# Output weights asked for earlier in the opening, and by another queue in the second half

## The chip, the cores and the metric

The kernel runs on one core of a Trainium2 chip, in one launch. A core has TensorE (PE: matrix products; its weight loads are PEld), VectorE (DVE), ScalarE (ACT), GpSimd (POOL) and SyncE (SP). SP, ACT and POOL also issue DMAs, each on a queue of its own; the transfers of all three run on the same 16 DMA engines. The metric is the device time in microseconds (us), of which lower is better.

## The reference, cut to what matters

The input x has 64 batches of 32 tokens of 512 values. Two layers follow one another, each added to its input:

```python
W = weights[condition]                       # one 32 x 32 matrix per batch
x = x + einsum('bct,bcd->bdt', x, W)         # mixes the 32 tokens of a batch

q = rope(rmsnorm(x @ Wq.T))                  # 32 heads of 128
k = rope(rmsnorm(x @ Wk.T))                  # 8 heads of 128, each for 4 heads of q
v = x @ Wv.T
k_all = concat(k_cache[block_table], k)      # 16 pages of 32 cached keys, and the 32 new ones
v_all = concat(v_cache[block_table], v)
probs = softmax(where(valid, q @ k_all.T / sqrt(128), -1e30))
x = x + (probs @ v_all) @ Wo.T               # Wo: 512 x 4096
```

All of it is in float32. The tables of pages and the lengths are inputs of the run.

## The kernel before, in words

**Tiling.** The heads are cut into two halves (16 heads of q, 4 of k and v in each). The tokens are cut into 16 tiles of 128, which is four batches each. A *step* is one tile in one half: steps 0 to 15 are the first half, 16 to 31 the second (`NT` is 16). The four batches of a step and the four heads of k make 16 *slots*, numbered 0 to 15; in each slot TensorE computes the scores of one batch and head against the 512 cached keys (`ps`, L570), ScalarE takes the exponential (`pr`), and one slot later TensorE multiplies with the values (`po`, L628). Around this, each step prepares the next one: in slots 3 to 7 TensorE projects k and q of the next step (`pp_k`, `pp_q`, L401), and VectorE normalizes and rotates them (a chain of some eight instructions for each q) and writes them to `rows`. In slots 9 and 11 SP *spreads* them by DMA from `rows` to `q_cols` (batches 0 to 2 of the step) and `q_last` (batch 3), four DMAs per batch, L465. In slots 8 and 9 TensorE does the output projection of the step before (`pout`, L516), with the output weights `wo`. In slots 14 and 15 it mixes and turns the x of the step after the next (`pmix`, `px1t`); ScalarE copies the result to `x1t` and stores it to memory for the second half (`x1t_d`, L368, issued by ACT). At the start of a step come the scores and values against the new keys (`psn`, L588, and `pnv`, L612): `psn` reads the queries and keys of all four batches of its step, so it needs the whole spread.

**The opening.** Step 0 has no step before it. All that it needs is written out in a fixed order of its own: projections, two batches of scores and the first fills, up to slot 4 of step 0, where the loop takes over.

**Keys and values.** The keys of a batch come as 16 pages, one DMA of 64 KB for each page, issued by SP (`k_t`, L291), into two buffers; `Batch(...)` issues them, two batches ahead. VectorE copies them head by head to `kh` (L563), which frees the buffer. The values come in four chunks of 256 KB for a batch, each gathered by an indirect DMA of POOL (`raw`, L315) into three buffers; ScalarE masks a chunk into `v` (L328), which frees its buffer for the next gather.

**Output weights.** `wo` of one half is four tiles of 1 MB. `load_parts` asks for half a tile, in two DMAs of 256 KB, each of which fills 32 partitions (L249). There is one set of tiles for both halves: the second half's weights may come only when the last projection of the first half has read the tile.

**Fallback.** The exponentials are taken without subtracting a maximum; at the end a count of the denominators decides whether a second, exact pass runs. It doesn't in the runs shown.

**Order.** SP and TensorE do their work in the order in which the program writes it. ACT, VectorE and POOL are ordered by a scheduler, after the opening. Each engine issues and waits in its order: what stands behind a waiting instruction waits too. The table that places the loads of `wo` by step and slot is:

```python
        output_weights = {
            (0, 4): (0, 1),
            (0, 5): (2, 3),
            (0, 6): (4, 5),
            (1, 4): (6,),
            (1, 5): (7,),
            (NT, 10): (0,),
            (NT + 1, 2): (1,),
            (NT + 1, 4): (2,),
            (NT + 1, 5): (3, 4),
            (NT + 1, 6): (5, 6),
            (NT + 1, 7): (7,),
        }
```

Of the kernel before, what the change touches and what calls it, by code (L numbers as in the profile page):

```python
# [20 lines left out]
B, S, HID = 64, 32, 512  # L21
# [7 lines left out]
NT = B // BT  # L29
NHH = 2  # L30
GH = HK // NHH
# [24 lines left out]
def cond_resid_paged_attention_kernel(  # L56
# [23 lines left out]
    nc = tc.nc  # L80
# [101 lines left out]
    def run(exact):  # L182

        with ExitStack() as pools:
            steps_of(exact, pools)

    def steps_of(exact, pools):
# [46 lines left out]
        def load_w(kind, hh, g=0, part=slice(0, 4), eng=nc.sync):  # L234
            if kind == "q":
                src = wq[:, (hh * QH + g * REP) * D : (hh * QH + (g + 1) * REP) * D]
            elif kind == "o":
                src = wo[(hh * QH + g * REP) * D : (hh * QH + (g + 1) * REP) * D, :]
            else:
                src = (wk if kind == "k" else wv)[:, hh * GH * D : (hh + 1) * GH * D]  # L240
            if part.start == 0:
                wt[kind, hh, g] = wpool.tile(
                    [P, 4, 512], F32, tag=f"w{kind}{g}", name=f"w{kind}{g}_{hh}_{uid}"
                )
            t = wt[kind, hh, g]
            if kind == "o" and not exact:
                src = src.rearrange("(h j p) e -> h p j e", h=REP, p=S)
                for h in range(part.start, part.stop):
                    nc.sync.dma_start(t[h * S : (h + 1) * S, :, :], src[h])  # L249
                return  # L250
            eng.dma_start(t[:, part, :], src.rearrange("(c p) e -> p c e", p=P)[:, part, :])

        def load_parts(which, hh, at):

            if 0 <= at < 2 * len(which):
                load_w(which[at // 2][0], hh, which[at // 2][1], slice(at % 2 * 2, at % 2 * 2 + 2))

        def load_cond_weights(t, eng=nc.sync, kind=mybir.EngineType.SP):
            _, number = nc.values_load_multi_w_load_instructions(
# [234 lines left out]
        def k_b(st):  # L494
            to_columns(st, GH)
# [58 lines left out]
        def queries(ba, g):  # L554
            return columns(ba.st, ba.bt)[:, g, :]

        def head_keys(ba, g, eng=None):

            k = work.tile([P, NPP, PSIZE], F32, tag="kh", name=f"kh_{ba.name}_{g}", bufs=4)
            if eng is nc.scalar:  # L560
                nc.scalar.copy(k, ba.k_raw[:, :, g, :])
            else:
                last["dve"] = nc.vector.tensor_copy(k, ba.k_raw[:, :, g, :]).ins  # L563
            ba.k[g] = k.rearrange("p j r -> p (j r)")

        def scores(ba, g):

            ps = ps_s.tile([P, VC, P], F32, tag="ps", name=f"ps_{ba.name}_{g}")
            for c in range(VC):
                nc.tensor.matmul(  # L570
                    ps[:, c, :],
                    ba.k[g][:, c * P : (c + 1) * P],
                    queries(ba, g),
                    start=True,
                    stop=True,
                )
            pr = work.tile([P, VC, P], F32, tag="pr", name=f"pr_{ba.name}_{g}", bufs=3)
            last["act"] = nc.scalar.activation(pr, ps, AF.Exp, scale=SCALE).ins  # L578
            ba.pr[g] = pr
# [241 lines left out]
        head_keys(batch, 2, nc.scalar)  # L821
        head_keys(batch, 3, nc.scalar)
        scores(batch, 0)
        after = Batch(first, 2)
        k_b(first)
        for c in (0, 1):
# [34 lines left out]
        def pieces(st):  # L861
            do = {
                2: (rot_tables,),
                3: (k_a,),
                4: ((q_a, 0),),
                5: ((q_a, 1),),
                6: ((q_a, 2),),
                7: ((q_a, 3),),
                9: ((spread, (0, 1, 3)),),
                11: ((spread, (2,)),),  # L870
                13: (v_a,),
            }
            if st is second:
                do[2] = do[3] = do[13] = ()
            return do
# [14 lines left out]
        def next_values():  # L890
# [7 lines left out]

        x1_a(steps[2])
        load_cond_weights(2)  # L900
        output_weights = {
            (0, 4): (0, 1),
            (0, 5): (2, 3),
            (0, 6): (4, 5),
            (1, 4): (6,),
            (1, 5): (7,),
            (NT, 10): (0,),
            (NT + 1, 2): (1,),
            (NT + 1, 4): (2,),
            (NT + 1, 5): (3, 4),  # L910
            (NT + 1, 6): (5, 6),
            (NT + 1, 7): (7,),
        }
        for st in steps:
            ahead = steps[st.n + 1] if st.n + 1 < len(steps) else None
            beyond = steps[st.n + 2] if st.n + 2 < len(steps) else None
            fill = pieces(ahead) if ahead else {}
            for bt in range(0 if st.n else 1, BT):
                this, after = batch, None
                n = st.n * BT + bt + 2  # L920
                if n < NHH * NT * BT:
                    after = Batch(steps[n // BT], n % BT)
                    unfilled += [(after, c) for c in range(VC)]
                for g in range(GH):
                    slot = bt * GH + g
                    if st.n or slot > GH:
                        scores(this, g)
                    if slot == 0:
                        new_scores(st)
                    if slot in (1, 3):  # L930
                        new_values(st, slot - 1)
                    if slot < GH and valued is not None:
                        values(*valued)
                    for piece in fill.get(slot, ()):
                        if isinstance(piece, tuple):
                            piece[0](ahead, piece[1])
                        else:
                            piece(ahead)
                    if slot in (8, 9) and st.n:
                        out_proj(steps[st.n - 1], slice((slot - 8) * QH // 2, (slot - 7) * QH // 2))  # L940
                    if slot == 9:
                        if st.n:
                            new_ot(st)
                        for ba in turned:
                            turn(ba)
                        turned = []
                        if 0 < st.n < NT // TRIG - 1:
                            tmp = work.tile(
                                [P, 3, TRIG * HD], F32, tag="w1", name=f"trig_{st.n}", bufs=1
                            )  # L950
                            with tc.issue_after(last["dve"]), tc.issue_after(last["act"]):
                                angles((st.n + 1) * TRIG, tmp)
                    if slot == 10 and st.n:
                        store(steps[st.n - 1])
                    if st.n and beyond:
                        if slot == 6 and not beyond.hh:
                            load_cond_weights(beyond.t)
                        if slot == 11:
                            x1_a(beyond)
                    if slot == 13 and beyond:  # L960
                        x1_t(beyond)
                    if slot == 14 and beyond:
                        x1_c(beyond)
                    if slot == 15 and beyond:
                        x1_b(beyond)
                    if slot == 1 and st.n == NT:
                        count(0)
                    for at in output_weights.get((st.n, slot), ()):
                        load_parts([("o", i) for i in range(GH)], st.hh, at)
                    if st.n in (NT - 2, NT - 1):  # L970
                        load_parts(
                            [("k", 0), ("q", 0), ("q", 1), ("q", 2), ("q", 3), ("v", 0)],
                            1,
                            slot - 5 + (st.n - NT + 2) * BT * GH,
                        )
                    for _ in range({1: 0, GH: 2}.get(slot, 1)):
                        if unfilled and (g or unfilled[0][0] is this):
                            next_values()
                    if slot >= GH and valued is not None:
                        values(*valued)  # L980
                    valued = this, g
                    if g == 1 and bt != 1:
                        for ba in turned:
                            turn(ba)
                        turned = []
                    if later is not None:
                        head_keys(later, g)
                turned.append(this)
                batch, later = later, after
# [75 lines left out]
```

## Time and profile before

| what | value |
|---|---|
| time, median of 3 runs | 2191.49 us (2189.07 to 2192.82) |
| the profiled execution: its time | 2190.95 us |
| the profiled execution: its span, first to last instruction | 2189.2 us |
| PE busy | 2151.3 us, 98% |
| VectorE, ScalarE, POOL busy | 55%, 40%, 37% |
| DMA: mean rate over the span | 164 GB/s |
| granted TensorE clock, mean | 0.992 |
| SP's issues of k_t, q_cols and q_last, wo | 2048, 372 and 124, 32 |
| POOL's gathers raw | 512 |

A line of a timeline gives the start and the length in us, the engine, the line of the kernel, the operation, what it writes and reads, how many instructions are merged, and in brackets the idle time before it and what ended that. A line of the waits gives the engine and line that waited, who released it, the sum in us, the number of waits and the longest. SPq, ACTq and POOLq are the issuing sides of these engines. The names end in `_x` where buffers have numbers.

### The profile page before, as it was taken

Reading aid. Unit: us, or ns where it says so; the run is one execution under the profiler, and the core shown is the slowest. Engines: PE = TensorE matmul, PEld = TensorE weight load, DVE = VectorE, ACT = ScalarE, POOL = GpSimd, SP = SyncE. Lnnn points to the kernel's source line nnn. Section 1 sums busy time; section 2 is a strip of 40 time slices with the busy share of each in tenths; the row PEclk is TensorE's granted clock in tenths of the full one; section 3 lists DMA queues with packets and bytes.
Section 4 is the critical chain, followed back from the end, with each engine's and each line's share of the span. In section 5 each row is a group of like instructions: output and inputs, shape, how many; then the busy total and the mean of one; then the engine's idle time right before and its main releaser. Section 6 shows DMA issues by size and latency. Waiting matters only on the chain.

```text
span 2189.2 us, 41546 instructions
## 1 busy us (share of the span) xinstructions
PE 2151.3 (98%) x12970; PEld 1500.0 (69%) x12970; DVE 1199.7 (55%) x2881; ACT 867.3 (40%) x1574; POOL 806.1 (37%) x1008
## 2 busy tenths in 40 slices
PE   8879999999999999999999999999999999999998
PEld 5657766677766777667777667777667776667775
DVE  5555566655565545556545656445556445656442
ACT  3434444444333443334443334443334443334441
POOL 4433333433343333334333434333334334334330
PEclk9989999999999999999999999999999999999999
DMA  7656555555555555556856865555555655555652
GB/s 227 175 157 176 150 154 145 167 163 159 161 144 158 161 169 154 153 151 189 252 166 173 206 169 160 169 162 163 147 162 160 173 162 155 151 162 161 175 153 62
DMA packets 387863, 358.77 MB, mean 164 GB/s; under 512 B 54737, under 2 KB 316897, under 8 KB 387633
## 3 DMA queue, kind: packets, MB, share of 16 engines
q1 hardware_dynamic: 342912, 215.10, 35.0%
q0 software_dynamic: 41712, 136.66, 21.8%
q10 hardware_dynamic: 3008, 4.25, 0.5%
q8 instruction: 106, 1.74, 0.3%
q14 instruction: 125, 1.02, 0.2%
HBM read 302.59 MB, written 12.58 MB: 144 GB/s over the span
## 4 chain that ended last, share of the span: by engine, by line
PE 97%; DMA 1%; SPq 1%; issue 0%; ACT 0%; DVE 0%; ACTq 0%; DVEq 0%
PE po_x L628 22%; PE ps_x L570 21%; PE pout_x L516 20%; PE pp_q_x L401 20%; PE pp_v_x L401 5%; PE pp_k_x L401 5%; PE pnv_x L612 2%; PE psn_x L588 2%; PE pmix_x L357 1%; SPq L465 0%; DMA wq_x<-in_wq_dram 0%; SPq L291 0%; PE px1t_x L365 0%; DMA x1t_d<-x1t_x 0%; DMA w_sel<-in_w_cond_dram,cond 0%
## 5 line engine op out<-in xcount | busy, mean ns | idle before, releaser
L315 POOL DMA_INDIRECT raw_x<-in_vc_dram,v_row x512 | 539.8, 1054 | 840.3 <-ACT v_x L328 772.5
L578 ACT ACTIVATE pr_x<-ps_x 128x512 f32<-128x512 f32 x512 | 305.8, 597 | 833.8 <-PE ps_x L570 774.1
L628 PEld LDWEIGHTS po_x<-v_x,pr_x 128*128 128x128 f32 x4096 | 517.0, 192 | 125.6 <-issue 115.2
L628 PE MATMUL po_x<-v_x,pr_x 128*128 128x129 f32 x4096 | 552.3, 278 | 1.1 <-issue 1.1
L401 PE MATMUL pp_q_x<-wq_x,x1t_x 128*128 128x512 f32 x1024 | 463.4, 595 | 4.3 <-DMA wq_x<-in_wq_dram 4.3
L516 PE MATMUL pout_x<-wo_x,ot_x 128*128 128x512 f32 x1024 | 450.2, 592 | 0.0
L570 PE MATMUL ps_x<-q_cols_x,kh_x 128*128 128x128 f32 x3072 | 406.9, 275 | 13.1 <-DMA q_cols_x<-rows_x 12.6
L570 PEld LDWEIGHTS ps_x<-q_cols_x,kh_x 128*128 128x128 f32 x3072 | 377.4, 192 | 29.8 <-issue 28.3
L328 ACT ACTIVATE v_x<-raw_x,valid 128x512 f32<-128x512 f32 x512 | 363.0, 716 | 9.5 <-DMA raw_x<-in_vc_dram,v_row 9.5
L516 PEld LDWEIGHTS pout_x<-wo_x,ot_x 128*128 128x128 f32 x1024 | 189.7, 190 | 214.3 <-issue 214.0
L401 PEld LDWEIGHTS pp_q_x<-wq_x,x1t_x 128*128 128x128 f32 x1024 | 186.0, 192 | 190.2 <-issue 185.7
L563 DVE COPY kh_x<-k_t_x 128x512 f32<-128x512 f32 x506 | 206.2, 417 | 195.7 <-PE ps_x L570 159.1
L646 DVE TENSOR_TENSOR nv_x<-po_x,nv_x 128x258 f32<-128x258 f32 x256 | 108.4, 423 | 322.8 <-PE po_x L628 311.0
L418 POOL TENSOR_TENSOR rs_q_x<-ms_q_x,minus_half 128x4 f32<-128x4 f32 x128 | 140.7, 1099 | 176.2 <-DVE ms_q_x L416 176.2
L411 ACT ACTIVATE sq_q_x<-pp_q_x 128x512 f32<-128x512 f32 x128 | 76.6, 598 | 272.9 <-PE pp_q_x L401 171.2
L570 PE MATMUL ps_x<-q_last_x,kh_x 128*128 128x128 f32 x1024 | 135.1, 275 | 0.0
L524 DVE TENSOR_TENSOR acc_x<-pout_x,acc_x 128x512 f32<-128x512 f32 x32 | 22.1, 692 | 199.5 <-PE pout_x L516 199.5
L570 PEld LDWEIGHTS ps_x<-q_last_x,kh_x 128*128 128x128 f32 x1024 | 124.6, 192 | 0.0
L401 PE MATMUL pp_k_x<-wk_x,x1t_x 128*128 128x512 f32 x256 | 116.1, 596 | 0.0
L401 PE MATMUL pp_v_x<-wv_x,x1t_x 128*128 128x512 f32 x256 | 115.2, 592 | 0.0
L415 DVE TENSOR_REDUCE ms_q_x<-sq_q_x 128x4 f32<-128x512 f32 x128 | 86.6, 676 | 49.9 <-ACT sq_q_x L411 48.0
L649 DVE TENSOR_TENSOR o_x<-nv_x,rden 128x256 f32<-128x256 f32 x256 | 108.5, 424 | 6.5
(105 smaller groups left out, 1464.5 us busy)
## 6 DMA issues: line engine op xcount, KB each, us to landing
k_t_x<-in_kt_dram SPq DMA_DIRECT2D x2048, 64.0 KB
q_cols_x<-rows_x SPq DMA_DIRECT2D x372, 80.0 KB
q_last_x<-rows_x SPq DMA_DIRECT2D x124, 80.0 KB
raw_x<-in_vc_dram,v_row POOLq DMA_INDIRECT x512
wo_x<-in_wo_dram SPq DMA_DIRECT2D x32, 256.0 KB
acc_x<-in_x_dram SPq DMA_DIRECT2D x16, 256.0 KB
x1t_d<-x1t_x ACTq DMA_DIRECT2D x16, 256.0 KB
acc_d<-acc_x SPq DMA_DIRECT2D x16, 256.0 KB
```

What stands on the lines that cost most here:

```text
L315: nc.gpsimd.indirect_dma_start(out=raw.rearrange("p g d -> p (g d)"), out_offset=None, in_=vc, in_offset=bass.IndirectOffsetOnAxis(ap=v_ro ...
L328: nc.scalar.activation(v_bufs[b % 2][:, c, :, 0:D], raw, AF.Copy, scale=ok)
L401: nc.tensor.matmul(pp, st.x1t[:, c, :], w[:, c, :], start=(c == 0), stop=(c == KC - 1))
L415: nc.vector.tensor_reduce(ms, sq, AX.X, ALU.add)
L418: nc.gpsimd.tensor_tensor(rs, ms, minus_half, ALU.pow)
L516: nc.tensor.matmul(st.po, st.ot[:, i, :], wt["o", st.hh, i // 4][:, i % 4, :], start=(i == 0), stop=(i == QH - 1),)
L563: last["dve"] = nc.vector.tensor_copy(k, ba.k_raw[:, :, g, :]).ins
L570: nc.tensor.matmul(ps[:, c, :], ba.k[g][:, c * P : (c + 1) * P], queries(ba, g), start=True, stop=True,)
L578: last["act"] = nc.scalar.activation(pr, ps, AF.Exp, scale=SCALE).ins
L628: nc.tensor.matmul(ba.po[:, g % 2, :], ba.pr[g][:, c, :], ba.v_t[:, c, g, :], start=(c == 0), stop=(c == VC - 1),)
L646: nc.vector.tensor_tensor(t, ba.po, t, ALU.add)
L649: nc.vector.tensor_tensor(ba.o[:, both, :], t[:, :, 0:D], rd.unsqueeze(2).to_broadcast([P, 2, D]), ALU.mult,)
```

## The change

The loads of the output weights are placed anew. In the first half SP still issues them: parts 0 to 2 directly after the opening's first score (that is between the pages of batches 1 and 2), parts 3 to 5 ahead of the loop (between the pages of batches 2 and 3), and parts 6 and 7 in slots 4 and 5 of step 1, as before. In the second half POOL issues them instead of SP, one part at a time: in slots 10, 13 and 15 of step 16 and in slots 1, 3, 4, 5 and 6 of step 17. `load_parts` and `load_w` take the issuing engine as an argument.

```diff
-                    nc.sync.dma_start(t[h * S : (h + 1) * S, :, :], src[h])
+                    eng.dma_start(t[h * S : (h + 1) * S, :, :], src[h])
...
-        def load_parts(which, hh, at):
+        def load_parts(which, hh, at, eng=nc.sync):
 
             if 0 <= at < 2 * len(which):
-                load_w(which[at // 2][0], hh, which[at // 2][1], slice(at % 2 * 2, at % 2 * 2 + 2))
+                kind, g = which[at // 2]
+                load_w(kind, hh, g, slice(at % 2 * 2, at % 2 * 2 + 2), eng)
+
+        outputs = [("o", g) for g in range(GH)]
...
         scores(batch, 0)
+        for at in (0, 1, 2):
+            load_parts(outputs, 0, at)
         after = Batch(first, 2)
...
         load_cond_weights(2)
-        output_weights = {
...
-        }
+        for at in (3, 4, 5):
+            load_parts(outputs, 0, at)
+        second_outputs = [(0, 10), (0, 13), (0, 15), (1, 1), (1, 3), (1, 4), (1, 5), (1, 6)]
...
-                    for at in output_weights.get((st.n, slot), ()):
-                        load_parts([("o", i) for i in range(GH)], st.hh, at)
+                    if st.n == 1 and slot in (4, 5):
+                        load_parts(outputs, 0, slot + 2)
+                    if (st.n - NT, slot) in second_outputs:
+                        at = second_outputs.index((st.n - NT, slot))
+                        load_parts(outputs, 1, at, nc.gpsimd)
```

More of the change, by code (lines that the diff above doesn't have):

```diff
@@ L900, in steps_of @@
         load_cond_weights(2)
-        output_weights = {
[L902 to L912, printed above, removed]
-        }
+        for at in (3, 4, 5):
+            load_parts(outputs, 0, at)
+        second_outputs = [(0, 10), (0, 13), (0, 15), (1, 1), (1, 3), (1, 4), (1, 5), (1, 6)]
         for st in steps:
```

## The prediction

> **What bounds the kernel now.** I read the page's busy line first, then the waits of TensorE, then the timelines of TensorE and of SP's queue around the longest wait.
>
> ```profile
> PE 2151.3 (98%) x12970; PEld 1500.0 (69%) x12970; DVE 1199.7 (55%) x2881; ACT 867.3 (40%) x1574; POOL 806.1 (37%) x1008
> ```
>
> TensorE is busy for 98% of the span, so only its idle time, some 38 us, can be won. Its waits say where the large pieces lie:
>
> ```profile
> PE ps_x L570 <- DMA q_cols_x<-rows_x: 12.6, 1, 12.6
> PE psn_x L588 <- DMA q_cols_x<-rows_x: 5.3, 1, 5.3
> PE pp_q_x L401 <- DMA wq_x<-in_wq_dram: 4.3, 1, 4.3
> PE pmix_x L357 <- DVE bd L799: 2.4, 1, 2.4
> ```
>
> The first two belong to one place, the border of steps 0 and 1. No wait of TensorE is later than 125.25 us, and step borders repeat every 67.1 us in the first half and 65.9 us in the second: the second half has nothing to give. In TensorE's timeline the place is:
>
> ```profile
> 103.17 1.06 PE L628 MATMUL po_x<-v_x,pr_x 128*128 128x129 f32 x8
> 116.85 2.05 PE L570 MATMUL ps_x<-q_cols_x,kh_x 128*128 128x128 f32 x8 [12.62 <-DMA q_cols_x<-rows_x]
> 118.83 1.10 PE L588 MATMUL psn_x<-q_cols_x 128*32 128x128 f32 x4
> 125.25 0.61 PE L588 MATMUL psn_x<-q_cols_x 128*32 128x128 f32 x2 [5.33 <-DMA q_cols_x<-rows_x]
> ```
>
> From step 0's pmix (100.09) to the next pp_k (136.44) takes 36.35 us; the same pieces a step later (189.54 to 203.57) take 14.03. The place costs 22.3 us: 17.95 of waiting, the rest mostly the clock (window 120 to 125.2: granted 0.50). Both waits are for the spread of queries that SP issues, and SP's queue shows why it is late:
>
> ```profile
> 73.54 11.02 SPq L249 DMA_DIRECT2D wo_x<-in_wo_dram  x12
> ...
> 89.02 2.63 SPq L291 DMA_DIRECT2D k_t_x<-in_kt_dram  x3
> ...
> 106.51 1.36 SPq L291 DMA_DIRECT2D k_t_x<-in_kt_dram  x3
> ...
> 112.69 5.06 SPq L465 DMA_DIRECT2D q_cols_x<-rows_x  x8
> 117.80 2.49 SPq L465 DMA_DIRECT2D q_last_x<-rows_x  x4
> 120.38 2.43 SPq L465 DMA_DIRECT2D q_cols_x<-rows_x  x4
> ```
>
> SP's own waits between 60 and 140 us, and the issue on ACT that they name:
>
> ```profile
> SPq L291 <- DMA x1t_d<-x1t_x: 14.7, 1, 14.7
> ```
>
> ```profile
> 104.10 0.36 ACTq L368 DMA_DIRECT2D x1t_d<-x1t_x  x1
> ```
>
> Pages of batch 4 stop after four issues (86.98, then three from 89.02) and go on at 106.51. The built program's list of waits explains it: DMAs of SP and ACT take eight completion semaphores in turn, and each waits until the last DMA on its semaphore has landed. The fifth page drew the one that x1t_d of step 2 uses. That store leaves ACT at 104.10, after TensorE's transposes of slot 15 (102.74), and its completion is recorded at 106.50. So the weights are not the wait itself: by the order of issue, their number decides which transfer is tied to the store.
>
> **The change part by part.** (a) Twelve wo DMAs leave SP between the pages of batches 3 and 4. In the built changed program the store's semaphore then falls to the first q_last DMA of the spread. Pages of batch 4 are free from 85.3 on (last kh copy of batch 2): 16 at 0.515 us end at 94, eight q_cols at 0.63 us end at 99 and land near 101. ps at 104.1 finds them: the 12.6 us go. What is late next: q_last waits for the store, landed 106.5; then four q_last and four q_cols, 8 x 0.63 = 5.0, last landing 2.0 to 2.9 us after its issue at 110.9 (before: 2.0 in the quiet case, 2.9 for the last): 113.1. psn, in order behind one ps, starts at 105 and stops at its third matmul until then, 8 us. It resumed at 125.25 before: 12.1 us gained, and the path behind shifts as a whole. Batch 5's pages follow the spread as before (1.9 us after its last issue), so their distance to TensorE is kept.
>
> (b) Six of the twelve go before batch 2's pages, 6 x 0.48 = 2.9 us of SP from 41.3. In the new order it is the third of these pages, not the eighth, that waits for step 1's x1t_d (issued 49.51, landed 51.54), so 14 pages follow instead of 9: 5 x 0.51 = 2.6 us later. The first use of batch 2's keys comes behind two rounds of VectorE's rope work, near 81: hidden, with over 15 us to spare. Gathers issued 41.0 to 43.7 are wanted at 65.5 and land by 55 even behind 1.5 MB.
>
> (c) Six go before batch 3's pages. SP was free from 58.95 to 64.93; 2.6 + 2.9 us fit. But 1.5 MB now flow from about 64 on, and this meets a gather that has no slack:
>
> ```profile
> 70.07 0.72 ACT L328 ACTIVATE v_x<-raw_x,valid 128x512 f32<-128x512 f32 x1 [2.63 <-DMA raw_x<-in_vc_dram,v_row]
> ```
>
> It was issued at 66.50 and ACT already waits for it; behind it in ACT's order stand the square of q0 and with it VectorE's rope chains, busy 14.1 of 15 us in 72 to 87. In the changed order of VectorE the copies kh of batch 3 stand behind all four chains, behind the values of batch 2 (nv_x from po), where before they were slipped in between. ps of batch 3 starts at 94.30; undelayed, the copy ends near 94.5 (0.3 us lost). Each us by which the gather is late then goes to TensorE, less some 0.6 us of gaps in the chains. How late? The nearest rows are the same weights before: first to ninth wo landed 78.67 to 91.30 with two gathers between, ten blocks of 256 KB, 1.26 us each; the gather issued at 74.17 in the midst landed at 82.2, 8 us later, in about the order of issue. So six blocks from 64.1 end at 71.7 and the gather lands near 73 instead of 70: TensorE loses 3.0 - 0.6 + 0.3 = 2.7. If x1t_d of step 1 is itself slowed by the first lot, all is up to 2.5 us later: 5. The Trainium skill (DMA: Bandwidth & Descriptors, Queues, rings and completion order) says that each DMA engine takes turns between queue rows packet by packet; then the gather, on POOL's row, would share evenly with SP's backlog and land one block, 1.3 us, later: loss 1.0, and the sum would be -11.1. The trace's 8 us speaks against even turns, so I take 2.7 and keep 0.3 to 5.
>
> (d) The last four loads of the first half stay in step 1, slots 4 and 5: nothing.
>
> (e) Second half: 16 DMAs go from SP to POOL. No POOL row has this shape; pages_at and norm_q (128 rows each) took 0.60 and 0.61 us, wk (512 rows) 0.82. I take 0.6, 9.6 us in all, over 55 us in which POOL mostly waits (its wait for ACT v_x before gathers is 772.5 us over the run). The first waits for out_proj of step 15 to be done with its first four heads (near 1168; POOL arrives at 1170.3, after the gather of 1168.95), so nothing queues behind it for long. Behind them in POOL's order stand gathers, mask copies and rs; the tightest gather there, issued 1185.18, landed 1188.59 and was wanted at 1189.56, 1 us of slack; the next have 2.7 to 3.5. The two wo just before the tight one can go near 1178, when POOL is idle, and have landed. Cost 0; if one gather is late by a block more than its slack, 1 to 2 us. Removing the loads from SP gains 0: TensorE never waited. SP's last weights landed 1240.55 for a projection at 1240.68; on POOL they are issued by 1225.
>
> (f) Clock. After 8 us idle the array restarts at half speed, as after 125.25, where it took 4.3 us to full (granted clock). The trace grants the clock in steps of 3.4 us, which makes this 2.8 to 6.2 us at half speed: 1 us either way.
>
> **Sum.** -12.1 + 2.7 = -9.4 us. The profiled run took 2190.95 us around a span of 2189.2, and stands 0.5 us under the median 2191.49. From the median: 2182.1, said as 2182.
>
> **The rivals.** *The whole border heals* (-22.3 + 2.5 us, 2171.5): if q_last and the last q_cols land by 105. For it: SP could have issued them by 104. Against it: the store's semaphore stands before q_last in the built program, and the store can't leave before 104. Chance 0.07.
>
> *The opening eats the gain* (2189): the gather lands 7 us later still, TensorE loses 10 instead of 2.7, and -12.1 + 10 = -2.1. For it: VectorE is full there and the new order has no filler; a stall may also bring the half-speed clock (window 60 to 72: granted 0.86). Against it: it needs the gather at 80, beyond both lots' 3 MB. That the change does not do what it says, the store landing on yet another page, ends here too. Chance 0.12.
>
> *POOL's queue holds back the gathers of the second half* (slower, 2198): each of some eight gathers between 1183 and 1225 finds one or two 256 KB blocks before it, 1.3 to 2.5 us, and POOL's own waits on its eight semaphores. It decides where lateness passes the slack of 1.0 to 3.5 us; at 2 us over for eight gathers TensorE loses 16 us, -9.4 + 16 = +6.6. Against it: gathers of 9.7 us (issued 1223.42, landed 1233.16) behind SP's weights stalled nothing. Chance 0.06.
>
> **How the numbers follow.** Main case 0.75: ends of (c) give -12.1 + 0.3 to -12.1 + 5, with the clock -12.8 to -6.1, so 2178.7 to 2185.4. To hold the time 8 times in 10 the range reaches to the rivals on the slow side and takes in a us of noise: 2177 to 2188. A measurement here tells 0.2%, 4.4 us, from no change. Faster: 0.75 + 0.07 = 0.82; same 0.12; slower 0.06.
>
> **What would show it.** Right: TensorE's wait of 12.6 us gone; one wait of about 8 us at psn for q_cols; in SP's waits x1t_d before L468 (q_last) instead of before a page; a wait of 1 to 5 us at ps near 94; step borders at 65.9 us in the second half. Wrong: no wait at psn (whole border heals), long waits of ACT for raw_x past 75 us, or new waits of TensorE for v_x between 1185 and 1240.

## The result and the profile after

The changed kernel takes 2186.28 us (median of 8 runs, 2183.46 to 2193.16), the kernel before 2192.32 us beside it (8 runs). The ratio is 0.9969, 95% interval 0.9958 to 0.9980: by the ratio, which is worked out from all runs, 6.8 us faster, and by the medians 6.0, where 9.4 were forecast. (The differences below are taken from the ratios too; those of the medians lie within 2.4 us of them.) A second set of runs of the same two kernels gave 0.9963 (0.9950 to 0.9976). The profiled execution took 2188.01 us around a span of 2186.2 us.

Of the page of the changed kernel, the busy line:

```profile
PE 2150.5 (98%) x12970; PEld 1498.3 (69%) x12970; DVE 1199.1 (55%) x2881; ACT 866.9 (40%) x1574; POOL 813.1 (37%) x1024
```

PE and VectorE are as busy as before; POOL counts 16 instructions more, the 16 issues. What changed is the waiting. The waits of TensorE, changed kernel (lines are numbered 3 higher than before):

```profile
PE psn_x L591 <- DMA q_cols_x<-rows_x: 7.7, 1, 7.7
...
PE ps_x L573 <- DVE kh_x L566: 2.9, 1, 2.9
PE pp_k_x L404 <- DMA x1t_x<-x1t_d: 2.5, 1, 2.5
```

The 12.6 us of ps for q_cols are gone, psn waits 7.7 us instead of 5.3, and two waits are new: 2.9 us for VectorE's copy kh, in the opening, and 2.5 us for a load of x1t, in the second half. TensorE's timeline around the border of steps 0 and 1, and its place in the second half:

```profile
97.46 1.13 PE L573 MATMUL ps_x<-q_last_x,kh_x 128*128 128x128 f32 x8 [2.90 <-DVE kh_x L566]
...
107.59 1.05 PE L573 MATMUL ps_x<-q_cols_x,kh_x 128*128 128x128 f32 x8
108.57 0.41 PE L591 MATMUL psn_x<-q_cols_x 128*32 128x128 f32 x4
116.72 0.60 PE L591 MATMUL psn_x<-q_cols_x 128*32 128x128 f32 x2 [7.74 <-DMA q_cols_x<-rows_x]
...
1200.99 5.37 PE L404 MATMUL pp_k_x<-wk_x,x1t_x 128*128 128x512 f32 x8 [2.45 <-DMA x1t_x<-x1t_d]
```

SP's queue in the same kernel, and its longest wait between 60 and 140 us:

```profile
64.49 2.79 SPq L249 DMA_DIRECT2D wo_x<-in_wo_dram  x6
...
68.58 28.47 SPq L294 DMA_DIRECT2D k_t_x<-in_kt_dram  x32
97.23 6.51 SPq L468 DMA_DIRECT2D q_cols_x<-rows_x  x8
...
110.22 2.41 SPq L468 DMA_DIRECT2D q_last_x<-rows_x  x4
112.72 2.43 SPq L468 DMA_DIRECT2D q_cols_x<-rows_x  x4
```

```profile
SPq L468 <- DMA x1t_d<-x1t_x: 6.5, 1, 6.5
```

The pages of batch 4 now go in one run with those of batch 3, the first eight gathers of the spread start at 97.23 instead of 112.69, and the store x1t_d (issued 107.62, landed 110.20) stands before the first q_last. The last of the spread lands at 116.63 and psn goes on at 116.72.

Where the time went is read from the starts of pp_k's first matmul, the borders of steps: pp_k of step 2, the first behind the border of steps 0 and 1, starts at 127.27 instead of 136.44, 9.2 us earlier. Steps 2 to 14 take 67.1 us as before. Steps 15, 17 and 18 take 66.4, 68.5 and 67.6 us where each took 65.8 or 65.9: 4.9 us are given back by the start of pp_k of step 19, 1.7 of them in step 18, which has a window of 3.4 us at half clock (granted clock 0.50) from 1201.7. The other steps of the second half take 65.9. A last 1.0 us goes behind the last pp_k, where a po waits 1.6 us for pr at 2133.19; the profile before has no such wait. So these two profiled executions differ by 2.9 us only. The sizes of gains and losses are therefore taken from all runs, and the profiles show the places.

### The profile page after: what moved, and what is told of

Same layout as the page of the kernel before. It is cut to its first block, busy times and chain, and to the rows that moved or that the text cites. A ratio compares the mean times of both kernels' runs of the same rounds, so it can differ in the third digit from the quotient of the medians.

```text
span 2186.2 us, 41553 instructions
## 1 busy us (share of the span) xinstructions
PE 2150.5 (98%) x12970; PEld 1498.3 (69%) x12970; DVE 1199.1 (55%) x2881; ACT 866.9 (40%) x1574; POOL 813.1 (37%) x1024
## 4 chain that ended last, share of the span: by engine, by line
PE 95%; DMA 2%; issue 1%; DVE 1%; ACT 0%; SPq 0%; POOL 0%; ACTq 0%; DVEq 0%; POOLq 0%
PE po_x L631 21%; PE ps_x L573 20%; PE pout_x L519 20%; PE pp_q_x L404 19%; PE pp_k_x L404 5%; PE pp_v_x L404 5%; PE pnv_x L615 2%; PE psn_x L591 1%; DMA raw_x<-in_vc_dram,v_row 1%; PE pmix_x L360 1%; DMA pages_at<-in_pages_v_dram 0%; DMA x1t_x<-x1t_d 0%; DMA k_t_x<-in_kt_dram 0%; PE px1t_x L368 0%; SPq L468 0%
```

## Experiments

Parts 0 to 2 of the first half's weights are called the first lot below, parts 3 to 5 the second. For each profile two stretches are compared: from the second pp_k (which projects k for step 1, at 45 to 51 us) to the pmix of step 2, which is the opening's own work, and on to the next pp_k behind the border. The second pp_k is taken as zero since it moves between executions: it came at 45.3 to 46.3 us in three profiles (e1, e4, e10) and at 48.2 to 51.4 in the others. The difference arises at about 30 us, and the first load that an edit moves is issued at 40.6 us. At about 30 us pp_q waits for the weights wq 1.4 to 2.4 us in those three and mostly 2.7 to 4.3 in the others, and a half-speed window that follows there in the others is missing; what makes the weights land sooner or later was not found. Single times of one kernel differ by several us with this, so the ratios rest on several rounds of runs.

| kernel | ratio to before (95%) | second pp_k to pmix | to pp_k behind the border | loss behind step 15 |
|---|---|---|---|---|
| before | 1 | 50.2 | 86.6 | none |
| changed | 0.9969 (0.9958 to 0.9980) | 54.5 | 78.2 | 4.4 |
| a2, changed again | 0.9963 (0.9950 to 0.9976) | 52.7 | 77.0 | 8.1 |
| e1 first half only | 0.9956 (0.9947 to 0.9966) | 49.4 | 74.4 | 1.5 |
| e2 second half only | 1.0015 (1.0008 to 1.0023) | 48.9 | 85.8 | 7.2 |
| e3 store by POOL alone | 0.9954 (0.9935 to 0.9972) | 50.2 | 75.7 | 3.3 |
| e4 = e1 + store by POOL | 0.9948 (0.9929 to 0.9967) | 49.3 | 73.6 | 1.0 |
| e5 second lot late | 0.9977 (0.9966 to 0.9988) | 47.9 | 73.2 | 0.8 |
| e6 POOL's slots moved | 0.9965 (0.9952 to 0.9978) | 49.6 | 74.1 | 8.2 |
| e8 = e4, second lot late | 0.9916 (0.9903 to 0.9929) | 50.2 | 71.8 | 8.5 |
| e9 weights held around x1t | 0.9970 (0.9958 to 0.9981) | 52.4 | 76.7 | 3.9 |
| e10 x1t's load earlier | 0.9963 (0.9949 to 0.9976) | 48.6 | 77.3 | 1.9 |
| e12, e10 again | 0.9966 (0.9955 to 0.9977) | 55.0 | 78.3 | 4.1 |
| e11 all together | 0.9932 (0.9918 to 0.9945) | 49.4 | 69.6 | none |

(All but the ratios are of one execution each, in us. The last column is what steps 15 to 30 take in sum above the usual step of the same execution, 65.83 to 65.93 us; set against the steps of before, the changed kernel's is 4.9. The variants were measured in four sets, e1 to e4, then a2, e5, e6 and e8, then e9 to e11, and e12, each beside its own runs of the kernel before and with 5 to 22 runs each.)

**e1, the first half of the change alone.** As the changed kernel, but the second half's weights are issued by SP at the slots of before:

```diff
...
-                    if (st.n - NT, slot) in second_outputs:
-                        at = second_outputs.index((st.n - NT, slot))
-                        load_parts(outputs, 1, at, nc.gpsimd)
+                    for at in second_outputs.get((st.n - NT, slot), ()):
+                        load_parts(outputs, 1, at)
```

> The change in the first half alone; SP issues the second half's weights as before. Theory: the border of steps 0 and 1 gave 9.1 us in the profile of the whole change, and the loss of 4 us lies in the second half, where the load of x1t for step 18 stood behind POOL's weights. So this kernel is 8 to 9 us faster than before (about 2183.5), its second half has no wait of TensorE and steps of 65.9 us. Rival: the second half's loss has nothing to do with the queue (noise of single runs); then this equals the whole change, 6 us faster.

Measured: 2179.09 us beside 2188.95, 0.9956, which is 9.6 us faster. Of the waits of TensorE, e1:

```profile
PE psn_x L591 <- DMA q_cols_x<-rows_x: 8.6, 2, 7.5
...
PE ps_x L573 <- DVE kh_x L566: 1.0, 1, 1.0
...
PE pp_k_x L404 <- DMA x1t_x<-x1t_d: 0.9, 1, 0.9
```

The sum that was forecast for the whole change, -9.4, is what its first half does. The second half is not as free of waits as was expected: pp_k of step 19 waits 0.9 us for its x1t, and step 18 takes 66.9 us.

**e2, the second half alone.** Before's placement in the first half, the changed one in the second (the reverse of the edit of e1).

> The change in the second half alone; the first half's weights in slots 4 to 6 of step 0 as before. Theory: slower than before by 2 to 4.5 us (2194.5 to 2196.8), with a wait of pp_k for x1t near 1210 and a step of 67 to 69 us after it. Rival (the prediction's step e): no cost, 0 us.

Measured: 2192.76 us beside 2188.95, 1.0015, which is 3.3 us slower than before. The border waits are those of before, and there is one new wait, here the third line of TensorE's waits in e2:

```profile
PE ps_x L573 <- DMA q_cols_x<-rows_x: 12.4, 1, 12.4
PE psn_x L591 <- DMA q_cols_x<-rows_x: 5.3, 1, 5.3
PE pp_k_x L404 <- DMA x1t_x<-x1t_d: 4.8, 1, 4.8
```

So the two halves act apart and add up: -9.6 + 3.3 = -6.3, measured -6.8. What the second half costs is where the change fell short.

**a2, the changed kernel again.**

> The changed kernel again, on the same chip as its variants, to have more runs of it. Expected as before: ratio 0.9969 to the kernel before (0.996 to 0.998), which is e1's 0.9956 plus what the second half's transfers on POOL cost (e2 alone: +0.0015). In the profile: one slow step border in the second half, pp_k waiting for x1t_x with the output weights of POOL on the DMA engines ahead of it.

Measured: 0.9963. The wait on x1t_x is there again, 5.5 us, in the same step (before it had been 2.5), with 6.8 us at half clock: it belongs to the change, its size varies.

**e3, the store by POOL.** Before, with one edit: the store of step 2's x1t, whose completion the pages of batch 4 had to wait for, is issued by POOL, and so takes no semaphore in the turn of SP and ACT.

```diff
-            nc.scalar.dma_start(x1t_d[st.t], st.x1t.rearrange("p c q -> p (c q)"))
+            eng = nc.gpsimd if st.n == 2 and not exact else nc.scalar
+            eng.dma_start(x1t_d[st.t], st.x1t.rearrange("p c q -> p (c q)"))
```

> Before, with one edit: the store of x1t of step 2 is issued by POOL, whose DMAs have completion semaphores of their own; all weights stay where they were in before. Theory (the semaphore): the fifth page of batch 4 no longer waits for the store; pages go out by about 98, the spread by 106, psn waits 3 to 4 us instead of 18 in all, and the kernel is 15 to 18 us faster (about 2175). Rival (bandwidth: the pages are late since 3 MB of weights flow before them): at most 3 us faster.

Measured: 0.9954, 10.1 us faster (6 to 14 by the interval) with the weights exactly where they were. SP's queue in e3:

```profile
80.41 1.25 SPq L249 DMA_DIRECT2D wo_x<-in_wo_dram  x2
83.64 14.39 SPq L291 DMA_DIRECT2D k_t_x<-in_kt_dram  x16
98.22 5.59 SPq L466 DMA_DIRECT2D q_cols_x<-rows_x  x8
103.85 2.80 SPq L466 DMA_DIRECT2D q_last_x<-rows_x  x4
106.75 2.46 SPq L466 DMA_DIRECT2D q_cols_x<-rows_x  x4
```

The pages of batch 4 no longer stop after the fourth. This settles step (a): the wait at the border was the tie of two DMAs by a semaphore, not the bytes of the weights (that rival allowed 3 us). The size was missed, -10 against -15 to -18. The stretch to the border is only 10.9 us shorter (75.7 against 86.6), since ps and psn still wait, 2.8 and 4.6 us, for a spread that SP issues at 0.63 us a piece behind the pages. And 3.3 us went in the second half, where one wait of TensorE is for a load of x1t:

```profile
PE pp_k_x L402 <- DMA x1t_x<-x1t_d: 2.6, 1, 2.6
```

This is not the load that is late in the changed kernel but the next, for step 19, and the second half's weights are with SP here. In the profile before, that load lands 1.2 us ahead of its pp_k. So little slack is used up without POOL's weights too: TensorE waits for the same load in e1 (0.9 us) and in e8 (4.2). What the move to POOL costs is therefore read from the many runs of e2 and of e1, and not from one profile.

**e4, both.** e1 with the store of e3.

> The first kernel of this call with the store of step 2 issued by POOL too. Theory: q_last no longer waits for the store; the spread ends near 109, psn waits about 2 us instead of 7.7, so 14 us faster than before (2178), 5.5 faster than the first kernel. What stays is the late gather of the opening (TensorE's wait at ps of batch 3, about 3 us, and for v). So it is about 2 us slower than the third kernel, which has no late gather. Rival (bandwidth): equal to the first kernel, or better than the third, since the weights are out of the way of the pages.

(In this text the first kernel is e1 and the third is e3.) Measured: 0.9948, 11.4 us faster where 14 were expected. That is 1.8 more than e1 and 1.3 more than e3, within the intervals. psn waits 6.8 us (5.3 the longest) instead of the expected 2: psn had been reached at 100.7, SP issues its last q_cols at 103.95, and it lands at 107.92. With the tie gone, SP's rate of issue is the next limit, and the landing comes on top: 4.0 us for this q_cols, where most of the spread in the profile before landed in 2.0 to 2.1.

**e8, the second lot out of the way.** e4 with parts 3 to 5 not ahead of the loop but in slots 1 to 3 of step 1:

```diff
-        for at in (3, 4, 5):
-            load_parts(outputs, 0, at)
...
-                    if st.n == 1 and slot in (4, 5):
+                    if st.n == 1 and 0 < slot < 6:
                         load_parts(outputs, 0, slot + 2)
```

> e4 (first half as changed, second half by SP, store of step 2's x1t issued by POOL) with parts 3 to 5 moved to slots 1 to 3 of step 1: the order of VectorE in the opening is as in e4, no semaphore ties the spread to the store in either, so what differs is the second lot between 64 and 75 us alone and six issues of SP. Theory (the lot delays a gather and with it the opening): 1 to 4 us faster than e4, ratio 0.993 to 0.9943. Rival (the pages of batch 4 wait for VectorE's copies anyway, so SP's six issues and the lot are hidden): ratio 0.9948 as e4. The wait at psn stays at 5 to 7 us by both, as the spread's last gather is set by SP's issue rate behind the pages.

Measured: 2176.45 us beside 2194.47, 0.9916: 18 us faster than before, and its interval ends where that of e4 begins. psn waits 4.1 us instead of 6.8, though its wait was expected to stay. The theory is right in sign, but its 1 to 4 us were too few beside the 7 between the ratios, and the profiles show only 1.8 of them (71.8 against 73.6 us to the border); the two kernels were measured in different sets, and where the rest comes from is not shown. The profiled execution is the slowest of the five, 2185.88 us where the others took 2174.87 to 2177.67, so the 8.5 us in the table's last column are not what this kernel loses as a rule.

**e5, the second lot late, the store left with ACT.** e1 with parts 2 to 5 in slots 0 to 3 of step 1 (8 DMAs instead of e8's 6).

> e1 (first half as changed, second half by SP as before) with parts 0 and 1 before batch 2's pages and parts 2 to 5 only in step 1, slots 0 to 3: no weights on the DMA engines from 64 to 75 us, and VectorE's copies kh of batch 3 again between the rope chains. The store's semaphore falls to the third q_last instead of the first: 2 issues of 0.63 us less behind it. Theory (the second lot makes a gather late in most executions, and TensorE loses up to 3 us by it; e1's profile with its early opening was a lucky one): 1.3 + 1 to 3 us faster than e1, ratio 0.994 to 0.9947. Rival (the lot does not matter, since the gathers are issued ahead of it when the opening runs early): only the 1.3 us, ratio 0.995; and with kh's copies between the chains it could be nothing: 0.9956.

Measured: 0.9977, slower than e1 (0.9956), which neither theory allowed. The stretch to the border is 1.2 us shorter than in e1 (73.2 against 74.4), the rival's 1.3, but the next step takes 73.6 instead of 67.1. TensorE's timeline in e5:

```profile
181.37 2.04 PE L360 MATMUL pmix_x<-acc_x,bd 128*128 128x512 f32 x2 [3.45 <-issue]
```

and SP's queue in e5:

```profile
131.29 3.75 SPq L249 DMA_DIRECT2D wo_x<-in_wo_dram  x8
136.32 14.84 SPq L294 DMA_DIRECT2D k_t_x<-in_kt_dram  x16
151.21 1.85 SPq L249 DMA_DIRECT2D wo_x<-in_wo_dram  x4
...
177.99 0.34 SPq L348 DMA_DIRECT2D acc_x<-in_x_dram  x1
```

At the end of this queue stands the load of acc that pmix needs: issued at 177.99, landed at 181.17, and pmix starts at 181.37. The profile gives the wait to "issue", which means that it found no releaser; the landing 0.2 us before the start points to this load. 6.8 us at half clock follow. In e8, with 6 loads behind the border instead of 8, the same load went out at 167.27 and step 2 took 67.2. So the room on SP's queue for loads behind this border lies between 6 and 8 of them, as far as these two profiles show.

**e6, POOL's slots moved.** The changed kernel with parts 5 to 8 at later slots of step 17:

```diff
-        second_outputs = [(0, 10), (0, 13), (0, 15), (1, 1), (1, 3), (1, 4), (1, 5), (1, 6)]
+        second_outputs = [(0, 10), (0, 13), (0, 15), (1, 1), (1, 5), (1, 6), (1, 7), (1, 8)]
```

> The changed kernel, except that the second half's parts 5 to 8 (of eight) are put on POOL's queue at slots 5 to 8 of step 17 instead of 3 to 6: POOL then issues none of them between about 1189 and 1200 us, where SP's load of x1t for step 18 is on its way. Theory (the loss of the second half is this one load standing behind POOL's blocks on the DMA engines): the load lands within 4 us of its issue, the wait of pp_k for x1t_x and the half-speed clock after it go, steps of 65.9 throughout, and the time is that of e1, ratio 0.9956: 3 us below the changed kernel. Rival (the weights hurt wherever they are on POOL's queue, by its gathers or by sharing engines with the spread): ratio stays at 0.997, with waits of TensorE for v_x or q_cols_x in steps 17 and 18. Also possible: the weights now come too late for the projection at slots 8 and 9, seen as pout waiting for wo_x.

Measured: 0.9965, unchanged, and nothing follows for the theories: POOL's queue came out in nearly the same order, with two wo issued at 1189.3 and 1189.9 just ahead of the load of x1t at 1190.37. The slot in the source did not fix the place on POOL's queue, which the scheduler makes.

**e9, the weights held around the load.** The changed kernel with parts at slots (0,10) to (0,13) and (1,4), (1,5), each behind the last gather written before it:

```diff
...
-        second_outputs = [(0, 10), (0, 13), (0, 15), (1, 1), (1, 3), (1, 4), (1, 5), (1, 6)]
+        second_outputs = {(0, 10): (0,), (0, 11): (1,), (0, 12): (2,), (0, 13): (3,), (1, 4): (4, 5), (1, 5): (6, 7)}
...
-                    if (st.n - NT, slot) in second_outputs:
-                        at = second_outputs.index((st.n - NT, slot))
-                        load_parts(outputs, 1, at, nc.gpsimd)
+                    for at in second_outputs.get((st.n - NT, slot), ()):
+                        with tc.issue_after(last["gather"]):
+                            load_parts(outputs, 1, at, nc.gpsimd)
```

> The changed kernel with the second half's parts on POOL held behind gathers in POOL's order, so that four parts are issued before the load of x1t for step 18 is asked for (until about 1180 us), none from there to its landing, and four from about 1200 us on. Its own e6 had only moved slots in the source; the order on POOL's queue, which the scheduler makes, stayed as it was. Theory (the load stands behind POOL's blocks of weights): it lands within 5 us, pp_k of step 18 waits under 1 us, no half-speed window near 1200, the step takes 65.9 to 66.9 instead of 68.5 to 71.6: 2 to 4 us faster than the changed kernel, ratio 0.995 (0.9942 to 0.996). Rival (what counts is the bytes that share the engines in these steps, not who stands ahead): unchanged, 0.9965.

Measured: 0.9970, no gain. In the profile the load does what the theory says: issued at 1195.73, landed at 1198.86, 3.1 us instead of 7.6, and pp_k of step 18 no longer waits. But there is another wait in TensorE's timeline of e9:

```profile
1192.85 0.49 PE L631 MATMUL po_x<-v_x,pr_x 128*128 128x129 f32 x2 [1.66 <-ACT v_x L331]
```

and in POOL's timeline what stands ahead of these values:

```profile
1177.23 1.13 POOL L249 DMA_DIRECT2D wo_x<-in_wo_dram  x2
1178.67 1.01 POOL L318 DMA_INDIRECT raw_x<-in_vc_dram,v_row  x1 [0.30 <-issue]
1179.67 1.13 POOL L249 DMA_DIRECT2D wo_x<-in_wo_dram  x2
...
1181.17 1.02 POOL L318 DMA_INDIRECT raw_x<-in_vc_dram,v_row  x1 [0.16 <-issue]
```

Now the gathers of 1178.67 and 1181.17 stand among six blocks of weights (two more were issued from 1174.79 on); they landed after 10.4 and 10.9 us. With its half-speed window the step lost 3.9 us. This is the prediction's third rival (POOL's queue holds back the gathers), with one wait of TensorE instead of eight.

**e10 and e12, the load itself earlier.** The changed kernel; in the second half the v projection is done at slot 11 instead of 13, which frees the buffer of x1t, and the load follows at once, ahead of 16 pages.

```diff
+            if st.n > NT:
+                do[11], do[13] = (*do[11], v_a), ()
...
+                    if slot == 11 and st.n >= NT and beyond:
+                        x1_t(beyond)
...
-                    if slot == 13 and beyond:
+                    if slot == 13 and beyond and st.n < NT:
```

> The changed kernel with the load itself moved instead of the weights: in the second half the projection of v for the next step is done at slot 11 instead of 13, which frees the buffer of x1t, and SP is given the load of x1t right then, ahead of the 16 pages of keys that it stood behind. Weights on POOL's queue as changed. Theory (the load is late because it is asked for late, and then stands behind the weights): it is issued some 8 to 12 us before pp_k needs more than now, no wait of pp_k on it in any step, second half 65.9 throughout: 3 to 5 us faster than the changed kernel, ratio 0.9945 to 0.9955. Rival (the weights only move their harm to the pages or gathers behind them): waits of TensorE for kh_x or v_x in steps 17 and 18, ratio 0.9965.

> e10 again (the changed kernel with the load of x1t asked for some 17 us earlier), because five runs left it open whether the harm of the weights on POOL's queue is gone: 0.9963 (0.9949 to 0.9976) against 0.9966 of the changed kernel. Theory (the wait for x1t_x and the half-speed clock behind it are the whole of what the second half lost): 3 us below the changed kernel, ratio 0.995 to 0.996. Rival (the weights harm something else in these steps as well): 0.9965 to 0.997, and a wait of TensorE in steps 16 to 18 that the profile of e10 did not show.

Measured: 0.9963 and 0.9966, the changed kernel's own ratio. SP's queue in e12:

```profile
1179.50 0.34 SPq L354 DMA_DIRECT2D x1t_x<-x1t_d  x1
1179.94 0.38 SPq L348 DMA_DIRECT2D acc_x<-acc_d  x1
1181.60 4.43 SPq L294 DMA_DIRECT2D k_t_x<-in_kt_dram  x7
```

It is asked for 17.9 us ahead of its pp_k; in the changed kernel it was 5.3 us ahead of the moment at which pp_k began to wait. Steps 16 to 24 take 65.8 in both profiles, so the wait on x1t in these steps is healed. But both lose time in step 25, where before lost none: 1.3 us in e10, 3.8 in e12. TensorE's timeline and ACT's, e12:

```profile
1720.22 1.24 PE L615 MATMUL pnv_x<-vn_x,pn_x 32*128 32x129 f32 x16 [2.17 <-ACT pn_x L599]
```

```profile
1716.13 0.72 ACT L331 ACTIVATE v_x<-raw_x,valid 128x512 f32<-128x512 f32 x1 [2.16 <-DMA raw_x<-in_vc_dram,v_row]
```

A gather there is issued at 1712.26, 2.6 us later than a step before it in the same place (1643.85 + 65.83 = 1709.68), and ACT, in order, holds the rest behind it. Why the order of ACT and POOL differs in this one step is not shown; e11, which has the same early load but the weights with SP, does not lose there. The profiles show that the load of x1t was the place of the loss in steps 17 and 18. That removing it gains time is not shown, for no version with the weights on POOL's queue came out free of a loss.

**e11, all together.** e8 with the early load of e10; the second half's weights are with SP.

> e8 (parts 0 to 2 before batch 2's pages, parts 3 to 5 in step 1, store of step 2's x1t by POOL, second half's weights by SP as before) and the load of x1t moved ahead as in e10. e8's profile still had 4.2 us of waiting for x1t_x in the second half, 4.4 + 2.5 us of longer steps with the clock. Theory: these go, all steps of the second half at 65.9, ratio 0.9895 to 0.991, against 0.9916 of e8. Rival (e8's waits on x1t were one execution's): as e8, 0.9916; what stays in the opening is the wait of 4 us at psn and the half-speed clock after it.

Measured: 2173.45 us beside 2189.76, 0.9932 (0.9918 to 0.9945): 15 us faster than before, less than the 0.9895 to 0.991 expected. By its own profile it is the cleanest: TensorE waits nowhere between 140 and 2170 us, and two of the waits that are left lie between the first projections and the border:

```profile
PE psn_x L592 <- DMA q_cols_x<-rows_x: 4.0, 1, 4.0
...
PE pnv_x L616 <- ACT nv_x L624: 1.0, 1, 1.0
```

Whether it is better or worse than e8 (0.9916) stays open: they ran beside different sets of the kernel before, and the intervals overlap. Both beat the two kernels given.

## Why the prediction was right, and where it was not

The time lies in the stated range of 2177 to 2188 us, and the border's gain came by the way that was described. One term of the sum was wrong, the second half's cost of 0 in step (e), which measured 3.3 us. That the range held all the same is in part luck: its slow end had been widened for rivals that did not come, and it took in a cost that was not foreseen. It is luck in part, too, that e1's -9.6 meets the sum of -9.4 so closely: in e1's profile the gather of (c) lands in time, so that the 2.7 us are not paid, and 1.5 us are lost in the second half.

**(a) The tie.** Right, in mechanism and size. "psn ... stops at its third matmul until then": it does, with a wait of 7.7 us (8.1 in a2, 7.5 in e1) where 8 was said. It resumes at 116.72 in the profile, and at 115.02 in a2; the forecast's 113.1 plus the 2.7 us of step (c) makes 115.8. e3, which moves one store and no weights, shows that the tie is the cause.

**(b) The first lot.** Hidden, as said: SP's pages of batch 2 end at 61.5 us instead of 56.0. That is 2.9 more than the 2.6 forecast, 2.0 of it because the store x1t_d of step 1, for which the third page waits, lands at 53.5 instead of 51.5, behind the first lot. No wait of TensorE is for these keys; between 50 and 74 us it waits 1.0 us, as before.

**(c) The late gather.** Right where it happens, and it does not always happen. The gather was issued at 65.74, behind three blocks of the second lot, and landed at 74.01; the forecast said 73. ACT's timeline in the changed kernel and in e1:

```profile
74.03 0.72 ACT L331 ACTIVATE v_x<-raw_x,valid 128x512 f32<-128x512 f32 x1 [7.36 <-DMA raw_x<-in_vc_dram,v_row]
```

```profile
66.69 0.72 ACT L331 ACTIVATE v_x<-raw_x,valid 128x512 f32<-128x512 f32 x1 [2.86 <-DMA raw_x<-in_vc_dram,v_row]
```

In e1 the same gather went out at 62.89, ahead of the lot at 64.31, and landed in 3.8 us. The first half has the same edits in the changed kernel, a2, e1, e6, e9, e10 and e12, and the table's third column splits as the gather does: issued after the lot began (changed, a2, e9, e12) the opening takes 2.2 to 4.8 us more than before; issued first (e1, e6, e10) 0.7 to 1.7 less. The forecast's 2.7 lies in the first group; that POOL and SP race here, and that three profiles of seven would lose nothing, was not in it. As to the rule of the Trainium skill that was weighed there (DMA: Bandwidth & Descriptors, Queues, rings and completion order: turns between queue rows, packet by packet): the gather landed 8.3 us after its issue, 4.5 later than the gather of e1, and not one block of 1.3 us later, which was the estimate for even turns. From 65.7 to 74.0 us SP's queue moved 1.53 MB and POOL's 0.26. But the delay does not follow the number of blocks ahead either: it took 7.2 us behind four (a2), 6.9 behind two (e9) and 7.4 behind one (e12).

**(d) The loads left in step 1.** They cost nothing, as said: the steps behind the border take 67.1 us.

**(e) The second half.** This step failed. "Cost 0" measured 3.3 us (e2). The step counted what stands behind the weights on POOL's own queue, the gathers, and found slack for them; POOL's issues cost what was said, 0.56 to 0.64 us each. It left out SP's queue, whose pages and load of x1t share the DMA engines with POOL's transfers. In POOL's timeline of the changed kernel:

```profile
1188.35 0.60 POOL L249 DMA_DIRECT2D wo_x<-in_wo_dram  x1
1189.25 0.98 POOL L318 DMA_INDIRECT raw_x<-in_vc_dram,v_row  x1 [0.30 <-ACT v_x L331]
1190.94 0.95 POOL L318 DMA_INDIRECT raw_x<-in_vc_dram,v_row  x1 [0.70 <-ACT v_x L331]
...
1192.29 1.19 POOL L249 DMA_DIRECT2D wo_x<-in_wo_dram  x2 [0.18 <-issue]
```

and SP's queue in the changed kernel, then in the kernel before:

```profile
1181.67 11.47 SPq L294 DMA_DIRECT2D k_t_x<-in_kt_dram  x16
1193.25 0.37 SPq L354 DMA_DIRECT2D x1t_x<-x1t_d  x1
```

```profile
1189.75 9.07 SPq L291 DMA_DIRECT2D k_t_x<-in_kt_dram  x16
1198.84 0.33 SPq L351 DMA_DIRECT2D x1t_x<-x1t_d  x1
```

Before, the load was issued 7.9 us ahead of its pp_k (1206.76), took 3.6 us, and so had 4.3 us of slack. In the changed kernel two delays used this up. First, the 16 pages ahead of it took 2.4 us longer to issue: two of them waited for earlier pages, which landed late, as SP's waits between 1181 and 1194 us show:

```profile
SPq L294 <- DMA k_t_x<-in_kt_dram: 1.8, 2, 1.3
```

So the load was issued only 5.3 us ahead of the moment at which pp_k began to wait. Second, it took 7.6 us itself (landed at 1200.85), with five blocks of 256 KB from POOL still under way, three of weights and two of values, beside seven of SP's own pages of 64 KB. 2.6 us later and 4.0 us longer, less the slack of 4.3, makes 2.3; the wait was 2.45. In e2, a2 and e6 the load took 9.5 to 10.0 us. The slack of 4.3 us was to be read in the profile of before, one line of SP's queue beside one of TensorE's. "Removing the loads from SP gains 0" held for the profile before, where TensorE never waited; that SP's placement has a tight load of its own, the one for step 19, shows in e3.

**(f) The clock.** Inside the 1 us allowed at the border: the half-speed window there was 6.8 us (112.9 to 119.7), mostly in the wait. It was not allowed for elsewhere: the stop of 2.5 us in the second half was followed by a window of its own, and so a wait of 2.5 us cost 4.3 with the step behind it (68.5 and 67.6 above 65.9).

**The rivals.** The whole border did not heal: that needs the store out of the way, and even e4, where it is, keeps 6.8 us at psn. (The forecast's 2171.5 for this rival is a slip of the sum; its terms make 2171.7.) The opening did not eat the gain: it lost 2.2 to 4.8 us in the executions with the late gather, not 10. POOL's queue holding back gathers was seen only in e9, where the edit put more weights ahead of them.

## What to carry to other kernels

A wait that names a DMA need not be for its bytes: look for what else its semaphore is shared with, and move the sharer (one store to another queue, e3) before moving megabytes. When transfers are moved to another queue, list every load with little slack on all queues in that stretch, not only those behind them on the new one, and count both what delays its issue and what slows its landing. An edit that clears one tight load may only pass the delay to the next tight one (e9, e10, e5), so the whole row of step borders is to be read, not the wait that was aimed at.

## What was not expected of the hardware

The same instructions, up to the second pp_k, took from 45.3 to 51.4 us in different profiles, more than most edits here are worth. A short stop of TensorE can cost more than itself, but does not always: stops of 1.7 us (e9), 2.2 (e12) and 2.5 (changed) each came with 3.4 us at half clock, and stops of 3.5 (e5) to 5.5 us (a2) with 6.8, so that 2.5 us became 4.3 (changed), 5.5 became 8.1 (a2) and 1.7 became 3.9 (e9); but after 2.6 us in e3 the clock stayed at full. What decides this is not shown. And two queues do not always share the DMA engines alike: in the opening SP's queue moved 1.53 MB while POOL's moved 0.26, although up to three gathers were under way on POOL's; from 1193.2 to 1200.9 us, while x1t was on its way, they moved 0.86 and 1.07 MB. In both places a load that met a backlog on the other queue landed some 4 us late.
